# Deformable layer of a four-layer kernel: vertical tent weights made from offsets that DMA lays on every lane

## The chip, the cores and the metric

One NeuronCore of a Trainium2 chip runs the whole program in one launch. The metric is device microseconds of that core, from one execution of the program. Several runs were timed, and one further execution was profiled; durations of single instructions come from the profiled one.

## What is computed

The program chains four layers, each added to its input after a group normalisation of it. Only the first is touched by the change, a deformable 3 x 3 convolution over x of shape 4 images x 128 channels x 128 x 128 pixels:

```
offset = einsum('bchw,oc->bohw', x, w_off) + b_off          # 4 groups x 9 taps x {dy, dx}
py = off[..., dy] + (ky - 1) + row;   px = off[..., dx] + (kx - 1) + column
y0, x0 = floor(py), floor(px);        wy1, wx1 = py - y0, px - x0
val = x at (y0, x0), (y0, x0+1), (y0+1, x0), (y0+1, x0+1), zero outside the image,
      weighted by (1-wy1)(1-wx1), (1-wy1)wx1, wy1(1-wx1), wy1 wx1
out = relu(einsum('bgckhw,ogck->bohw', val, w_def));        x = x + out
```

Each of the 4 groups of 32 channels has its own 9 pairs of offsets at each pixel. The bilinear weight of a sample at distance (dy, dx) from a pixel is the product of two tents, max(0, 1 - |dy|) and max(0, 1 - |dx|). The other layers are a scan along rows, a message layer and a triangle product with layer norms.

## The kernel before, in words

`deform_layer` works in 172 blocks: 4 images x 43 blocks of RY = 3 rows. It replaces the gather by matrix products. For a strip of RX = 4 columns and a block of 3 rows, all samples with offsets below one pixel lie in a patch of SY x SX = 5 x 6 pixels. A *lane* is one pixel of the patch in one group: 30 x 4 = 120 lanes, on 120 partitions.

**Sampling.** `sample` (L521) multiplies, for each of 33 strips, the pixels (`pixels`, lanes x 128 channels, block diagonal in the groups) with the tent weights `m` (lanes x 9 taps x 3 rows x 4 columns), and gives the sampled values in PSUM (`v_ps`). `keep_samples` (L531, L536) copies them to SBUF with ScalarE. `convolved` (L579) then makes the 3 x 3 convolution from the samples, a block later, and `finish` (L552) adds the input.

**Tent weights.** The weight on lane l is the product of a tent along y, made from the tap's dy, and one along x. Both come from TensorE: `places` holds each offset split in three bfloat16 parts, with the parts of max(0, offset) beside them and a row of ones, and `spread` holds small constant matrices that turn these 25 rows into the tents on 120 lanes. `spread_offsets` (L498) does a *round* of such matmuls: for one or two taps, three matmuls along y (one for each row of the block, 130 columns) and four along x (one for each column of a strip, 99 columns) for each tap. The contraction has 25 rows, so that two taps and two directions sit side by side in four row groups of the array. A block takes five rounds (`SLOTS`): two taps four times and one once. `tents` then copies the y tent out of PSUM with ScalarE (`ty`, L508) and multiplies it with the x tent on VectorE (`m`, L510), one tap at a time.

**Preparation.** `prepared` handles 16 rows of an image: it transposes them (L370), scales them and writes a table of pixels to DRAM (`tab`, L378 and L380), makes the offsets with one matmul for each 4 rows (L385 to L393), splits them into parts (L409 to L418), and stores the parts for 8 rows to DRAM (`off`, L423). `counted` takes the statistics of the next image on VectorE. These jobs are generators that advance by one step, or by two where the rows are less than 26 ahead, after each of the eight sample groups of a block.

**Order.** The order on each engine is the order of the program text (`manual_schedule`). In a block, for i = 0 to 7: the round for tents of the next block, the copies of the sample group before, a few convolution matmuls, the sample group i, the products of the round, statistics, a step of preparation. All these loads and stores are DMAs issued by SP, in program order: pixels of the next block (L465, 4 DMAs) at the start of a block, `xres` (L573), the `places` of the block after the next (L449, 8 DMAs) at i = 3, and table and offset stores where the steps come. SP's instructions carry eight semaphores in turn, so that a DMA waits for the one eight before it to have landed.

Of the kernel before, what the change touches and what calls it, by code (L numbers as in the profile page):

```python
# [18 lines left out]
P = 128  # L19
# [30 lines left out]
SLOTS = [(0, 6), (1, 7), (2, 8), (3, 5), (4,)]  # L50
# [130 lines left out]
def deform_layer(tc, c, small, x, w_off, b_off, w_def, x1, tabs, offs):  # L181
# [13 lines left out]
    NB = RY * PADW  # L195
    with ExitStack() as ctx:
        wp = ctx.enter_context(tc.tile_pool(name="l0w", bufs=1))
        ps_g = ctx.enter_context(tc.tile_pool(name="l0ps_g", bufs=1, space=PSUM))
        ps_t = ctx.enter_context(tc.tile_pool(name="l0ps_t", bufs=2, space=PSUM))
        ps_v = ctx.enter_context(tc.tile_pool(name="l0ps_v", bufs=2, space=PSUM))  # L200
# [3 lines left out]
        NPH = NPY + NPX  # L204
# [9 lines left out]
        spread = wp.tile([P, NPH, LANES], BF16, name="spread")  # L214
        places = [wp.tile([P, len(SLOTS), RY, OW], BF16, name=f"places_{i}") for i in range(3)]
# [4 lines left out]
        def rims():  # L220

            zero = two.tile([P, 2 * SX * P], F32, name="zero", tag="m")
            nc.vector.memset(zero, 0.0)
            zrow = zero[0 : NXB + 1]
            zoff = zero[0 : 2 * NL, 0 : NPART * OW].bitcast(BF16)
            zoff = zoff.rearrange("p (n l) -> p n l", n=NPART)
            for b in range(B):
# [14 lines left out]
                nc.scalar.dma_start(rows_[:, :, (S + 2) * OW :], zoff)  # L242

        def tables():

            awayi = two.tile([NG, NPH, LANES], I32, name="awayi", tag="x1c")
            for i in range(NPY):
                nc.gpsimd.iota(
                    awayi[:, i], pattern=[[0, NG], [1, SY], [0, SX]], base=-1 - i,
                    channel_multiplier=0,  # L250
                )
            for i in range(NPX):
                nc.gpsimd.iota(
                    awayi[:, NPY + i], pattern=[[0, NG * SY], [1, SX]], base=-1 - i,
                    channel_multiplier=0,
                )
            away = two.tile([NG, NPH, LANES], F32, name="away", tag="x1c")
# [3 lines left out]
                out=away, in_=away, pattern=[[0, NPH], [1, LANES]], compare_op=ALU.is_ge,  # L261
# [3 lines left out]
                out=away, in_=away, pattern=[[0, NPH], [-1, LANES]], compare_op=ALU.is_ge,  # L265
# [3 lines left out]
            for i, sign in enumerate((-1.0, 1.0, 1.0)):  # L269
                nc.gpsimd.memset(picks[:, i], sign)  # L270
# [17 lines left out]
            for t in (*pixels, parts):  # L288
                nc.gpsimd.memset(t, 0.0)
            yield  # L290
            picks16 = one.tile([NG, 3, P], BF16, name="picks16", tag="ve")
            nc.vector.tensor_copy(picks16, picks.rearrange("g k q r -> g k (q r)"))
            kinds = two.tile([NG, 3, NPH * LANES], BF16, name="kinds", tag="m")
# [10 lines left out]
            n = NPH * LANES // 3  # L304
            for h in range(3):
                if h % 2 == 0:
                    tp = ps_t.tile([P, 2, 512], F32, name="t_ps")
                at = slice(h * n, (h + 1) * n)
                for i in range(3):
                    nc.tensor.matmul(  # L310
                        tp[:, h % 2, 0:n], lhsT=picks16[:, i], rhs=kinds[:, i, at],
                        start=i == 0, stop=i == 2,
                    )
                nc.scalar.copy(to[:, at], tp[:, h % 2, 0:n])
# [43 lines left out]
        def prepared(b, y0):  # L358
# [6 lines left out]
            for h in range(0, RC, RO):  # L365
# [23 lines left out]
                off = one.tile([2 * NL, RO, S], F32, name="off")  # L389
# [14 lines left out]
                def high(t):  # L404
                    halves = t.rearrange("p r c -> p (r c)").bitcast(BF16)
                    return halves.rearrange("p (r c two) -> p r c two", r=RO, two=2)[:, :, :, 1]

                rest = one.tile([2 * NL, RO, S], F32, name="rest")
                nc.scalar.copy(to(0), high(off))  # L409
                nc.gpsimd.tensor_tensor(rest, off, high(off), ALU.subtract)  # L410
                flat = off.rearrange("p r c -> p (r c)")
                nc.vector.tensor_reduce(ranges[:, 0, n : n + 1], flat, AX.X, ALU.max)
                yield
                nc.vector.tensor_reduce(ranges[:, 1, n : n + 1], flat, AX.X, ALU.min)
                nc.scalar.copy(to(1), high(rest))
                nc.gpsimd.tensor_tensor(to(2), rest, high(rest), ALU.subtract)
# [4 lines left out]
                if p0:  # L421
# [5 lines left out]
                        parts,  # L427
# [5 lines left out]
        def shifted(b, d, k, n, row, count):  # L433

            ky, kx = divmod(k, 3)
            wide = (S + 4) * OW
            first = (d * NK + k) * NG * NPART
            whole = offs[b]
            return bass.AP(
                whole.tensor, whole.offset + first * wide + (row - ky + 2) * OW + 2 - kx,  # L440
                [[wide, NG * NPART], [NG * NPART * wide - 1, n], [1, count]],
            )

        def load_places(b, j):
            t = places[(b * NYB + j) % 3]
            for d in range(2):
                for q, slot, k, n in ((0, 0, 0, 3), (0, 3, 3, 2), (1, 0, 6, 3), (1, 3, 5, 1)):
                    p1 = 64 * d + 32 * q + 1
                    nc.sync.dma_start(  # L449
                        t[p1 : p1 + KROWS - 1, slot : slot + n].rearrange("p k r c -> p k (r c)"),  # L450
                        shifted(b, d, k, n, RY * j, RY * OW),
                    )
            if j + 1 == NYB:
                for d in range(2):
                    p1 = 64 * d + 33
                    nc.sync.dma_start(
                        last[p1 : p1 + KROWS - 1].rearrange("p k r c -> p k (r c)"),
                        shifted(b, d, 6, 3, PADW - 1, OW),
                    )
            return t  # L460
# [13 lines left out]
        def spread_offsets(src, slot, taps, rows):  # L474

            tps, todo = [], []
            for q in taps:
                tp = ps_t.tile([P, 2, 512], F32, name="t_ps")
                tps.append(tp)
                for d in range(2):  # L480
                    p0 = 64 * d + 32 * q
                    wide = OW if d else PADW
                    to = tp[0:LANES, d, 0 : rows * wide].rearrange("p (r c) -> p r c", c=wide)
                    mov = src[p0 : p0 + KROWS, slot]
                    if d == 0:
                        ph0 = 0 if rows == RY else RY
                        lot = [(ph0 + r, to[:, r], mov[:, r, 0:PADW]) for r in range(rows)]
                    else:
                        lot = []
                        for i in range(NPX):  # L490
                            cs = slice(i, OW, RX)
                            lot.append((NPY + i, to[:, :, cs], mov[:, :, cs]))
                    todo.append([(p0, *v) for v in lot])
            for i in range(max(map(len, todo))):
                for lot in todo:
                    if i < len(lot):
                        p0, ph, to, mov = lot[i]
                        nc.tensor.matmul(  # L498
# [197 lines left out]
        for i in range(NB_):  # L696
            multiply(advance(i + 1))
# [1149 lines left out]
```

## Time and profile before

| what | value |
|---|---|
| three runs, median (lowest to highest) | 5597.54 us (5583.1 to 5604.08) |
| the profiled execution's own time | 5593.57 us |
| its span, first to last instruction | 5591.7 us |
| granted TensorE clock in it, mean | 0.969 |
| copies `v` out of `v_ps`, L531 | 1376 of 522 ns on ScalarE |
| copies `ty`, L508 | 1548 of 491 ns on ScalarE |
| products `m`, L510 | 1548 of 557 ns on VectorE |
| offset sum on GpSimd, L393 | 128 of 1266 ns |
| pixel loads, L465 | 688 of 123.8 KB |
| loads of `places`, L449 | 1376 of 18.6 to 55.7 KB |
| stores of `off`, L423 | 64 of 891 KB |

How to read the profile: lines of groups give line, engine, operation, output <- input, and a count. In lists of waits, "PE a <- DVE b" is time that TensorE stood before instruction a until VectorE's b was done: microseconds in total, times, longest. In a table of stretches, each engine has its busy time in the stretch with the number of instructions in brackets, in the order PE, PE weight loads, VectorE (DVE), ScalarE (ACT), GpSimd (POOL); the last three columns are the granted clock, the DMA share (mean over 16 engines; packets that overlap on an engine can take it above 1) and GB/s. SPq is SP's queue, with the time that issuing a DMA took. "SP waits" is time in which SP stood in front of a DMA.

### The profile page before, as it was taken

How to read it: one execution, taken by the hardware profiler on the slowest of the kernel's cores; microseconds unless marked ns; L12 is line 12 of the kernel's file. 1: busy time of each engine (PE TensorE's matmuls, PEld its weight loads, DVE VectorE, ACT ScalarE, POOL GpSimd, SP SyncE). 2: the span in 40 equal slices, each digit the busy share in tenths (PEclk: the TensorE clock that was granted, in tenths of full speed). 3: DMA queues.
4: the chain of work that ended last, by engine and by line, in shares of the span. 5: the costliest groups of instructions: out<-in, count | busy, mean ns of one | idle time of the engine just before them, and what ended most of it. 6: DMA issues, size and time to landing. Idle time of an engine off the chain costs nothing. (4 is left out here: it accounts for less than half of the span.)

```text
span 5591.7 us, 112174 instructions
## 1 busy us (share of the span) xinstructions
PE 5190.3 (93%) x42401; PEld 4449.9 (80%) x42401; DVE 3067.1 (55%) x10362; ACT 2766.6 (49%) x5892; POOL 785.0 (14%) x682
## 2 busy tenths in 40 slices
PE   2899999999999999999999989999989889889897
PEld 1778888888888888888888879999957768667687
DVE  6544444554444644444433337888875663754745
ACT  1345555445554455554544432333346574664855
POOL 2022111001111011111100002222200110200202
PEclk9899999999999999999999989999989999999999
DMA  4555555555555546554534322233222451632715
GB/s 142 144 129 137 131 134 119 124 121 136 133 132 117 132 111 138 129 139 107 125 77 79 74 63 84 91 119 94 91 96 86 127 209 36 227 127 78 247 48 172
DMA packets 1138394, 671.45 MB, mean 120 GB/s; under 512 B 737133, under 2 KB 1003566, under 8 KB 1121206
## 3 DMA queue, kind: packets, MB, share of 16 engines
q1 hardware_dynamic: 1127664, 657.77, 44.9%
q8 instruction: 337, 5.52, 0.4%
q10 hardware_dynamic: 10182, 6.43, 0.4%
q14 instruction: 211, 1.73, 0.1%
HBM read 382.88 MB, written 281.11 MB: 119 GB/s over the span
## 5 line engine op out<-in xcount | busy, mean ns | idle before, releaser
L510 DVE TENSOR_TENSOR m<-ty,t_ps 120x390 f32<-120x390 f32 x1548 | 805.2, 557 | 1506.2 <-ACT ty L508 1505.0
L521 PEld LDWEIGHTS v_ps<-m,pixels 120*128 120x128 f32 x11352 | 1442.3, 194 | 86.3 <-issue 9.1
L521 PE MATMUL v_ps<-m,pixels 120*128 120x108 f32 (+1 forms) x11352 | 1467.8, 274 | 3.6 <-ACT v L531 3.5
L531 ACT COPY v<-v_ps 128x432 f32<-128x432 f32 x1376 | 718.8, 522 | 1278.3 <-PE v_ps L521 1275.4
L579 PE MATMUL conv_ps<-v,wdef 128*128 128x128 f32 (+2 forms) x5160 | 1306.5, 380 | 6.5 <-DVE x1c L552 6.0
L579 PEld LDWEIGHTS conv_ps<-v,wdef 128*128 128x128 f32 x5160 | 816.2, 193 | 256.5 <-issue 21.9
L508 ACT COPY ty<-t_ps 120x390 f32<-120x390 f32 x1560 | 688.3, 489 | 175.8 <-PE t_ps L498 168.3
L498 PE MATMUL t_ps<-places,spread 25*120 25x99 bf16 (+1 forms) x10836 | 520.2, 260 | 61.9 <-DVE m L510 38.2
L498 PEld LDWEIGHTS <-spread 25*120 25x120 bf16 x10896 | 338.9, 137 | 224.4 <-issue 124.4
L1605 PEld LDWEIGHTS proj_ps<-wcat,X 128*128 128x128 f32 x4096 | 476.9, 193 | 25.1 <-issue 24.2
L393 POOL TENSOR_TENSOR off<-off,koff 72x512 f32<-72x512 f32 x128 | 162.0, 1266 | 2305.2 <-DVE off L390 2227.2
L1605 PE MATMUL proj_ps<-wcat,X 128*128 128x128 f32 x4096 | 483.8, 277 | 0.1
L1072 ACT ACTIVATE rowT<-x1T_ps,t_x,s_x 128x128 f32<-128x128 f32 x512 | 192.4, 456 | 366.7 <-PE x1T_ps L1065 342.8
L1085 PE MATMUL m_ps<-carry,w 128*128 128x172 f32 x2286 | 361.4, 311 | 0.0
L1699 POOL TENSOR_TENSOR work<-work,gate 128x512 f32<-128x512 f32 x128 | 163.6, 1278 | 1308.4 <-DVE X L1430 842.1
L1085 PEld LDWEIGHTS m_ps<-carry,w 128*128 128x128 f32 x2286 | 345.4, 188 | 0.0
L1614 DVE TENSOR_TENSOR L<-proj_ps,work 128x256 f32<-128x256 f32 x256 | 108.7, 424 | 427.1 <-ACT work L1609 427.1
L1185 POOL TENSOR_TENSOR sum_h<-sum_h,x2c 128x512 f32<-128x512 f32 x128 | 163.0, 1273 | 1159.8 <-DVE x2c L1145 1159.8
L1609 ACT ACTIVATE work<-proj_ps 128x512 f32<-128x512 f32 x256 | 151.5, 597 | 294.4 <-PE proj_ps L1605 291.9
L1710 PE MATMUL out_ps<-outw,work 128*128 128x128 f32 x1024 | 187.6, 285 | 29.0 <-POOL work L1699 27.3
L1710 PEld LDWEIGHTS out_ps<-outw,work 128*128 128x128 f32 x1024 | 159.4, 196 | 40.5 <-POOL work L1699 39.9
L1419 PE MATMUL self_ps<-R,ws 128*128 128x512 f32 x256 | 148.4, 673 | 35.7 <-DVE X L1430 24.3
(236 smaller groups left out, 6561.7 us busy)
## 6 DMA issues: line engine op xcount, KB each, us to landing
pixels<-tab SPq DMA_DIRECT2D x688, 123.8 KB
xin<-in_x_dram SPq DMA_DIRECT2D x56, 1024.0 KB
off<-parts SPq DMA_DIRECT2D x64, 891.0 KB
tab<-rows SPq DMA_DIRECT2D x384, 128.0 KB
places<-off SPq DMA_DIRECT2D x688, 55.7 KB
x<-x1c SPq DMA_DIRECT2D x32, 1024.0 KB
x1rows<-x SPq DMA_DIRECT2D x128, 256.0 KB
x2T<-x2c SPq DMA_DIRECT2D x128, 256.0 KB
```

Of the source, the lines that this page charges most:

```text
L498: nc.tensor.matmul(to, lhsT=spread[p0 : p0 + KROWS, ph, :], rhs=mov, start=True, stop=True,)
L508: nc.scalar.copy(ty[:, 0:n], tp[0:LANES, 0, 0:n])
L510: nc.vector.tensor_tensor(m, ty[:, 0:n].rearrange("p (r c) -> p r c", c=PADW), tx, ALU.mult)
L521: nc.tensor.matmul(vp[:, h * n : h * n + rows * w].rearrange("p (k c) -> p k c", c=w), lhsT=pix[0:LANES, xb, :], rhs=m[:, :, RX * xb : RX ...
L531: nc.scalar.copy(v[:, :, c0 : c0 + 4 * RX].rearrange("p k (h c) -> p k h c", c=RX), vp[:, 0 : 4 * n].rearrange("p (h k c) -> p k h c", h=4 ...
L579: nc.tensor.matmul(pc[:, at : at + r1 - r0, :], lhsT=wdef[:, 3 * ky + kx, :], rhs=v[:, k0 + kx, r0:r1, kx : kx + S], start=m == 0, stop=m ...
L1072: nc.scalar.activation(rt[:, b, :], px[:, b, :], AF.Identity, bias=t, scale=s)
L1085: nc.tensor.matmul(to, lhsT=wgt, rhs=src[:, :, at : at + n], start=i == 0, stop=i + 1 == len(todo),)
L1185: nc.gpsimd.tensor_tensor(sum_h, sum_h, x2c[:, :, i], add)
L1605: nc.tensor.matmul(pp[:, j], lhsT=X[:, j0 + j, :], rhs=wcat[:, cols], start=True, stop=True)
L1699: nc.gpsimd.tensor_tensor(a, a, gt, ALU.mult)
L1710: nc.tensor.matmul(po[:, j], lhsT=a[:, j], rhs=outw, start=False, stop=True)
```

## The change

The y tents no longer come from TensorE. The offsets along y are also written to DRAM as float32 (`offys`, one store for each 4 rows, from a new tile `wide` into which the offsets are now made). For each block, twelve DMAs read them back with a source step of 0 over 30 partitions, so that each lane of a group holds the same offsets, into one of three tiles `tent` (120 lanes x 9 taps x 3 rows x 132 columns, float32). ScalarE then takes |offset + constant of the lane| in place, one instruction for each row (`across`); VectorE makes min(|..| - 1, 0) of the whole tile in place (`lowered`); and `tents` multiplies it in place with the x tent from PSUM, three taps at once. Both factors are negated, so their product is the weight. `places` keeps the x offsets only, in three row groups (one for each ky), loaded by three DMAs; a round of `spread_offsets` makes the x tents of three taps with 12 matmuls, and a block has three rounds. `off` is stored for the x half alone. PSUM: `t_ps` becomes one tile of three banks instead of two tiles of two; `v_ps` three tiles instead of two. The loads for the block after the next move from i = 3 to i = 1.

```diff
+        tent = [wp.tile([LANES, NK, RY, OW], F32, name=f"tent_{i}") for i in range(3)]
...
+                nc.sync.dma_start(
+                    offys[b][:, r0 * OW : (r0 + RO) * OW],
+                    wide[0:NL].rearrange("p r c -> p (r c)"),
+                )
...
-                        parts,
+                        parts[NL:],
...
+        def same_on_lanes(b, g, ky, row, count):
+
+            whole = offys[b]
+            return bass.AP(
+                whole.tensor,
+                whole.offset + (KS * ky * NG + g) * WIDE + (row - ky + 2) * OW + 2,
+                [[0, NS], [NG * WIDE - 1, KS], [1, count]],
+            )
...
-            t = places[(b * NYB + j) % 3]
-            for d in range(2):
-                for q, slot, k, n in ((0, 0, 0, 3), (0, 3, 3, 2), (1, 0, 6, 3), (1, 3, 5, 1)):
...
+            t = places[(b * NYB + j) % 2]
+            y = tent[(b * NYB + j) % 3]
+            for ky in range(KS):
+                for g in range(NG):
                     nc.sync.dma_start(
-                        t[p1 : p1 + KROWS - 1, slot : slot + n].rearrange("p k r c -> p k (r c)"),
-                        shifted(b, d, k, n, RY * j, RY * OW),
+                        y[g * NS : (g + 1) * NS, KS * ky : KS * (ky + 1)].rearrange(
+                            "p k r c -> p k (r c)"
+                        ),
+                        same_on_lanes(b, g, ky, RY * j, RY * OW),
                     )
...
+        def spread_offsets(todo, rows):
+
+            tp = ps_t.tile([P, KS, 512], F32, name="t_ps")
+            for i in range(NPX):
+                cs = slice(i, OW, RX)
+                for q, p0, src in todo:
+                    to = tp[0:LANES, q, 0 : rows * OW].rearrange("p (r c) -> p r c", c=OW)
+                    nc.tensor.matmul(
+                        to[:, :, cs], lhsT=spread[p0 : p0 + KROWS, i, :],
+                        rhs=src[p0 : p0 + KROWS, :, cs], start=True, stop=True,
+                    )
+            return tp
+
+        def across(n, r):
+            t = tent[n % 3][:, :, r]
+            nc.scalar.activation(t, t, AF.Abs, bias=lane_y[:, r : r + 1])
+
+        def lowered(t):
+            nc.vector.tensor_scalar(t, t, 1.0, 0.0, ALU.subtract, ALU.min)
 
         def tents(tp, m, rows):
 
-            n = rows * PADW
-            ty = two.tile([LANES, NB], F32, name="ty")
-            nc.scalar.copy(ty[:, 0:n], tp[0:LANES, 0, 0:n])
-            tx = tp[0:LANES, 1, 0 : rows * OW].rearrange("p (r c) -> p r c", c=OW)[:, :, 0:PADW]
-            nc.vector.tensor_tensor(
-                m, ty[:, 0:n].rearrange("p (r c) -> p r c", c=PADW), tx, ALU.mult
-            )
+            tx = tp[0:LANES, :, 0 : rows * OW].rearrange("p k (r c) -> p k r c", c=OW)
+            nc.vector.tensor_tensor(m, m, tx, ALU.mult)
...
             for i in range(NG_X):
-                if i == 3:
+                if i == 1:
                     load_row(n + 2)
-                todo = advance(NB_ * (n + 1) + DONE[i])
+                todo = []
+                if more and i in (2, 4, 6):
+                    todo.append((n + 1, i // 2 - 1, spread_row(n + 1, i // 2 - 1)))
...
-                multiply(todo)
...
+                for v_ in todo:
+                    multiply(*v_)
+                if more and i == 0:
+                    across(n + 1, RY - 1)
+                if more and i == 1:
+                    lowered(tent[(n + 1) % 3])
+                if n + 2 < len(blocks) and i in (6, 7):
+                    across(n + 2, i - 6)
```

## The prediction, as put on record before the changed kernel ran

> **What bounds the kernel now.** I read the page first: its span, the engines' shares and the slices, to see which part of the span the change reaches.
>
> ```profile
> span 5591.7 us, 112174 instructions
> PE 5190.3 (93%) x42401; PEld 4449.9 (80%) x42401; DVE 3067.1 (55%) x10362; ACT 2766.6 (49%) x5892; POOL 785.0 (14%) x682
> ...
> PE   2899999999999999999999989999989889889897
> DMA  4555555555555546554534322233222451632715
> ```
>
> The deformable layer fills the first 23 to 24 of the 40 slices (its last sampling copy ends at 3303 us). TensorE is busy there in nine tenths or more of each slice, VectorE and ScalarE in about half. DMA stands at about half too, against two tenths in the next layer. So a DMA that is added lands where DMA is already fullest.
>
> Next, TensorE's own waits, from 440 us (past the ramp) to 3300 us:
>
> ```profile
> PE t_ps L498 <- DVE m L510: 13.6, 26, 2.6
> ...
> PE t_ps L498 <- DMA places<-off: 3.0, 5, 0.7
> ```
>
> Under 25 us of waits in 2860 us: in this stretch the layer's time is TensorE's list of work. Between the small closing copies of `keep_samples` (L536), which mark the blocks, I count 54 blocks without preparation of offsets (median 16.7 us), 97 with it (mean 18.2), 13 in the ramp (mean 21.9, the first ones held by VectorE's statistics) and the blocks at the ends of images. Then the timeline of TensorE, to price one round of `spread_offsets`:
>
> ```profile
> 1515.31 0.27 PE L370 MATMUL img_ps<-ident,xin 128*128 128x128 f32 x1
> 1515.52 0.56 PE L498 MATMUL t_ps<-places,spread 25*120 25x130 bf16 x14
> 1516.00 1.34 PE L579 MATMUL conv_ps<-v,wdef 128*128 128x384 f32 x4
> 1517.18 1.04 PE L521 MATMUL v_ps<-m,pixels 120*128 120x108 f32 x8
> 1518.16 0.55 PE L498 MATMUL t_ps<-places,spread 25*120 25x130 bf16 x7
> 1518.64 1.13 PE L579 MATMUL conv_ps<-v,wdef 128*128 128x256 f32 x4
> ```
>
> A round of 14 small matmuls stands between the last transpose, started at 1515.31, and the convolution at 1516.00. The transpose's own turn is 0.11 (four in 0.60, the last 0.27 long), so the round costs 0.58 us. A round of 7 costs the same: the eighth v_ps starts at 1517.18 + 1.04 - 0.26 = 1517.96, its turn ends at 1518.07, the next convolution starts at 1518.64, so 0.57. A round has a price, whatever number of matmuls is in it.
>
> Last, what DMA can carry: stretches of the trace (the last two columns are DMA share and GB/s), and SP's timeline in one block.
>
> ```profile
> 1531.00:1535.40 4.40, 4.40 (x36) 3.25 (x36) 0.76 (x2) 2.33 (x5) 0.00 (x0) 1.00 0.76 214
> 1542.00:1544.50 2.50, 2.50 (x22) 2.45 (x21) 1.88 (x4) 1.54 (x4) 1.81 (x2) 1.00 1.26 165
> 1540.60:1558.60 18.00, 18.00 (x169) 15.00 (x173) 7.55 (x14) 9.78 (x21) 4.31 (x4) 1.00 0.65 148
> 3200.00:3216.70 16.70, 16.70 (x162) 14.39 (x161) 5.22 (x11) 8.04 (x18) 0.00 (x0) 1.00 0.33 64
> ```
>
> ```profile
> 1540.61 2.23 SPq L465 DMA_DIRECT2D pixels<-tab  x4
> 1542.94 0.66 SPq L573 DMA_DIRECT2D xres<-in_x_dram  x1
> 1543.64 3.45 SPq L449 DMA_DIRECT2D places<-off  x8
> ```
>
> The stretches are one store of offsets; one load of pixels; one block with preparation; one without. In the store only 12 of 16 engines work (share 0.76) and they move 214 GB/s; all 64 such stores are near it (432 packets of 2112 B, mostly in 4.6 to 5.0 us, so 180 to 200). SP issues a DMA of `places` every 0.41 us. Over 440 to 3300 us SP waits 648 us for TensorE before pixel loads: 3.9 us of spare time in each of 166 blocks.
>
> **The change, part by part.**
>
> TensorE. Five rounds a block become three (12 matmuls each, 36 instead of 63). At 0.58 that is 2 x 0.58 = 1.16 us a block, x 172 = 200 us; at each image's end three rounds become one, 8 x 0.57 = 5. If nothing else moved: -205 us.
>
> ScalarE. Nine copies `ty` of 0.49 us go (4.4 a block). Three Abs over 1188 elements come. Copies of 130 and 390 elements took 268 and 491 ns, so 0.86 ns an element and 157 ns fixed; with up to 0.2 for the bias (the 512-wide ACTIVATE at L373 took 786, the copies 600): 1.2 to 1.4 us each, 3.6 to 4.2 a block. No change.
>
> VectorE. Nine products of 557 ns (5.0) become three of 1188: from 291 and 557 ns at 130 and 390 elements, 1.4 each, 4.1. New is `lowered`, 3564 elements in float32: 3.7 us at the products' 1.02 ns an element, 1.9 at half of that; bf16 at L418 took 0.44. At most +2.8 on 7.6 us busy in an 18 us block. Behind it queue six bn_stats (1.3 us) and the first product. With one `t_ps` buffer instead of two, the second round (i=4, some 8 us into the block) waits for that product, due 7 to 9 us in: 0 to 1 us in the one block of five that counts statistics, up to 30 us; I take 10. PSUM's third `v_ps` buffer lets TensorE run about two sample groups (4 us) past a ScalarE that is held up.
>
> DMA: this decides. A block's tents are 120 lanes x 9 taps x 1584 B = 1.71 MB, in 12 loads of 90 packets. The pixels, the largest load now, are 0.51 MB. Out go half of `places` (0.17 MB) and half of the offset store. How fast will 1584-byte packets to 30 lanes run? From both sides: the row nearest in packet size is `xres` (1536 B, 128 lanes). Its packets took 65 to 79 ns at the median; 1080 of them on the 15 engines that such a load uses are 4.7 to 5.7 us. But the Trainium skill ("SBUF — State Buffer", Door 1: The DMA port swizzle) says that a transfer's rate hangs on how many of SBUF's 16 ports its partitions reach: 32 partitions, and 64 as well, reach eight, measured there at 189 GB/s for 1 MiB against 328 for 128 partitions. By that rule it is 9.1 us. The row that speaks for it is the store above, from 72 lanes, at 180 to 214. I take 200 GB/s: 8.6 us. No row shows 30 lanes reading one and the same DRAM row, as these loads do. That can't beat the packet time, and may be slower.
>
> Then the waits on SP. In SP's program of the changed kernel the store of `offy` waits for the tents' loads of the same image in flight to land, and in most blocks it follows them directly; all later DMAs queue behind it: table rows, offset store, next pixels. A small `places` load, issued at 1511.36, had landed at 1513.11, so about 1.4 us pass between the end of issuing and landing.
>
> The queue for two blocks with preparation (it runs one step per i, so about one `offy` a block, six `tab` and one offset store every two):
> - pixels 2 x 0.51 MB at 165 GB/s: 6.2; xres 1.0
> - tents 2 x 8.6: 17.2; places 2 x 0.17 MB at 200: 1.7
> - offy 2 x 0.4, and 2 x 1.4 for landing: 3.6
> - tab 6 x 0.61: 3.7; offset store 0.46 MB at 200: 2.3
> - xin and x1, 0.9 of 1 MB in 2.7 us (128 packets of 8192 B went at 48 per us): 2.4
>
> Together 38.1, or 19.0 us a block. TensorE would need 18.2 - 1.2 = 17.0. So these blocks become the queue's, +0.8 us each: 97 x 0.8 = +78. Blocks without preparation: 3.1 + 0.5 + 8.6 + 0.9 + 1.4 = 14.5 us, below TensorE's 15.5, so they gain: 54 x 1.16 = -63; the images' ends -12. In the ramp six blocks write two `offy` and six `tab` each: about 3 us more, +18; the first tents, before the first sample, +5. Abs waits for the tents on ScalarE at i=6; queued behind it are the copies out of `v_ps` and the scaling of table rows, for which SP then waits. The copies are covered by the 4 us above; for the rows I take 1 us in every fourth prepared block, +24. With VectorE's 10: 78 - 63 - 12 + 18 + 5 + 24 + 10 = +60, less about 10 where x1 stores overlap table issues: +50 us. The profiled execution took 5593.6 us (span 5591.7); the median of the runs is 5597.5, 4 us above. On the median: 5650.
>
> **Rivals.**
> 1. TensorE stays the bound (the other side). If the tents run at xres's packet rate, 10.4 us for two blocks in place of 17.2, the queue needs 31.3, or 15.7 a block, less than 17.0. The 205 us come through but for some 10 to 40 us of starts and waits: 5390 to 5430. The turning point is the tents' rate: +50 vanishes when two blocks' queue is 1.0 us shorter, that is at about 212 GB/s; at 260 the queue needs 34.1 for two and TensorE decides. For it: loads to lanes 0-59 and 60-119 may drift apart and share all ports, and the loads are free of the offset store's small rows. Against it: the store at 214, and how fixed that is.
> 2. The shared source row is a hot spot: 15 engines reading the same 1584 B. At 120 GB/s tents take 14.3, prepared blocks 24.7 and the others 20: +800 us. Nothing in the trace speaks for it; nothing shows a broadcast either.
> 3. VectorE or the single `t_ps` becomes the bound: at worst 7.6 + 2.8 of 17 us, so it can't set the pace; 30 us at most, inside the ranges.
>
> **How the numbers follow.** The queue sets the pace (tents at 175 to 220 GB/s), 5580 to 5820: 0.55, of which 0.12 within 0.5% (28 us, about what a measurement of this kernel tells from no change) and 0.01 faster. TensorE the bound or nearly, 5385 to 5565: 0.33. Hot spot, above 5820: 0.12. Faster 0.34, same 0.12, slower 0.54. The range leaves some 0.08 at each end: 5400 to 5850; the likeliest case alone has 5580 to 5820.
>
> **What would show it.** Right: t_ps rounds at 0.58 us, three a block; blocks without preparation at 15.5 us; with preparation near 19, TensorE waiting there for v_ps copies or `m`, ScalarE for the tents' DMA, SP on `offy` for tents; DMA share above 0.85 in such a block; tents near 200 GB/s. Wrong: prepared blocks at 17 us with TensorE full, or blocks without preparation above 16.7. That last would mean that the tents' loads alone take over 10 us.

## The result, and the profile after

The changed kernel took 5886.51 us, median of 4 runs (5877.17 to 5895.4); the kernel before, beside it, 5592.44 (5583.1 to 5604.08). The ratio is 1.0527, 95% interval 1.0508 to 1.0547: 294 us slower, where 50 slower was forecast, outside the range. The profiled execution has a span of 5875.4 us, 283.7 more than before.

The page after, with the slices:

```profile
span 5875.4 us, 103049 instructions
...
PE 5107.6 (87%) x37747; PEld 4411.5 (75%) x37747; DVE 3319.1 (56%) x9499; ACT 2687.0 (46%) x4850; POOL 797.2 (14%) x683
...
PE   2688889989889888899889997999998989889797
...
DMA  5778778787788787788787873323323171441715
```

The last sampling copy ends at 3584.8 us instead of 3303.3, so 281.5 of the 283.7 us lie in the deformable layer. There the row of PE has fallen from 9 to 8 and 9, and DMA has gone from 5 to 7 and 8. The stretches show the same in numbers; the first is 500 us of the layer, the second the loading of one block's tents alone:

```profile
2500.00:3000.00 500.00, 453.99 (x3504) 388.17 (x3502) 255.75 (x428) 231.44 (x381) 75.91 (x72) 0.92 0.81 187
...
3306.00:3313.00 7.00, 6.88 (x59) 5.51 (x58) 2.92 (x3) 1.57 (x3) 0.00 (x0) 1.00 0.92 202
```

TensorE is busy for 454 us (426 to 454 in the five such stretches from 500 on; 493 to 498 before) at a granted clock of 0.90 to 0.92 (0.97 to 1.00 before). The tents come at 202 GB/s; in the single microseconds in which nothing but tents moves, the median is about 195. The forecast's 200 GB/s is there. DMA's share is 0.92 while the tents come, and 0.8 over 500 us: as a whole it is not full.

By blocks, counted between the closing copies as in the forecast (us, mean; the same block numbers in both, sorted by the kernel before):

| blocks | before | after | together | forecast |
|---|---|---|---|---|
| 97 with preparation | 18.19 | 20.00 | +175 | +102 (78 and 24) |
| 54 without (median 16.7, now 18.0) | 16.97 | 18.45 | +80 | -63 |
| 13 in the ramp | 21.93 | 24.69 | +36 | +18 |
| 7 at images' ends | 26.4 | 25.2 | -8 | -12 |

The new instructions cost what was forecast (last number ahead of the second bar: mean ns of one; behind it idle time, and what ended it):

```profile
L531 DVE TENSOR_TENSOR tent<-tent,t_ps 120x1188 f32<-120x1188 f32 x516 | 715.9, 1387 | 600.7 <-PE t_ps L515 593.8
L523 ACT ACTIVATE tent<-tent,lane_y 120x1188 f32<-120x1188 f32 x516 | 665.0, 1289 | 607.1 <-DMA places<-off 296.7
L526 DVE TENSOR_SCALAR tent<-tent 120x3564 f32<-120x3564 f32 x172 | 355.0, 2064 | 675.1 <-ACT tent L523 463.1
```

Product 1.39 us, Abs 1.29, `lowered` 2.06. The column behind the second bar is the news: ScalarE idled 607 us in front of Abs, about as long as Abs itself ran. The waits of the layer past the ramp (440 to 3585 us), TensorE's, ScalarE's and SP's:

```profile
PE off_ps L394 <- ACT rows L382: 124.6, 35, 10.9
PE v_ps L540 <- ACT v L550: 80.9, 39, 7.4
PE t_ps L515 <- DVE tent L531: 72.7, 48, 3.6
...
ACT tent L523 <- DMA places<-off: 282.9, 68, 12.3
ACT tent L523 <- DMA tent<-offy: 116.2, 23, 11.5
...
SPq L499 <- PE v_ps L540: 261.5, 72, 14.5
SPq L423 <- DMA tent<-offy: 193.5, 113, 4.9
```

TensorE, which waited under 25 us for all of this before, now waits for table rows of ScalarE, for ScalarE's copies and for VectorE's product. Each of the three stands behind Abs, on ScalarE itself or on VectorE, which waits for it. ScalarE's wait named "places" is put down to the load that came last; Abs reads no `places`, and the tents' loads are issued between them. SP's last line is the store of `offy` behind the tents.

A block without preparation shows how it fits together. TensorE's timeline first: the eighth v_ps of a group starts at 3301.97 + 1.04 - 0.26 = 3302.75, its turn ends at 3302.86, the convolution starts at 3303.43. A round of 12 costs 0.57 us, as forecast. Then the block after it:

```profile
3301.97 1.04 PE L540 MATMUL v_ps<-tent,pixels 120*128 120x108 f32 x8
3302.94 0.56 PE L515 MATMUL t_ps<-places,spread 25*120 25x99 bf16 x12
3303.43 0.71 PE L598 MATMUL conv_ps<-v,wdef 128*128 128x128 f32 x4
...
3315.04 1.28 ACT L523 ACTIVATE tent<-tent,lane_y 120x1188 f32<-120x1188 f32 x1 [3.12 <-DMA tent<-offy]
3316.64 1.28 ACT L523 ACTIVATE tent<-tent,lane_y 120x1188 f32<-120x1188 f32 x1
3318.32 1.30 ACT L523 ACTIVATE tent<-tent,lane_y 120x1188 f32<-120x1188 f32 x1
3319.65 2.02 DVE L526 TENSOR_SCALAR tent<-tent 120x3564 f32<-120x3564 f32 x1 [5.90 <-ACT tent L523]
3321.77 1.39 DVE L531 TENSOR_TENSOR tent<-tent,t_ps 120x1188 f32<-120x1188 f32 x1
3323.22 0.56 PE L515 MATMUL t_ps<-places,spread 25*120 25x99 bf16 x12 [1.44 <-DVE tent L531]
```

The pixels of that stretch were issued from 3299.47 on, when TensorE had left the block before; then `xres`, then the tents. The last tents landed at 3314.97, 15.5 us later. The queue's part of a block is the forecast's 14.5 us, nearly. But TensorE has used up its block by then. From the landing to the second round it is 8.3 us more: three Abs with copies between them, `lowered`, product, in a row. The pixels of the next block wait for TensorE again, so this is a loop: SP issues when TensorE is done, and TensorE waits for what SP issued last.

### The profile page after: what moved, and what is told of

The parts are those of the page before. It is cut to its first block, busy times and chain, and to the rows that moved or that the text cites. A ratio compares the mean times of both kernels' runs of the same rounds, so it can differ in the third digit from the quotient of the medians.

```text
span 5875.4 us, 103049 instructions
## 1 busy us (share of the span) xinstructions
PE 5107.6 (87%) x37747; PEld 4411.5 (75%) x37747; DVE 3319.1 (56%) x9499; ACT 2687.0 (46%) x4850; POOL 797.2 (14%) x683
## 5 line engine op out<-in xcount | busy, mean ns | idle before, releaser
L540 PEld LDWEIGHTS v_ps<-tent,pixels 120*128 120x128 f32 x11352 | 1502.7, 201 | 195.4 <-ACT v L550 101.8
L540 PE MATMUL v_ps<-tent,pixels 120*128 120x108 f32 (+1 forms) x11352 | 1527.1, 282 | 95.3 <-ACT v L550 93.2
L598 PEld LDWEIGHTS conv_ps<-v,wdef 128*128 128x128 f32 x5160 | 861.7, 203 | 301.3 <-issue 62.4
L531 DVE TENSOR_TENSOR tent<-tent,t_ps 120x1188 f32<-120x1188 f32 x516 | 715.9, 1387 | 600.7 <-PE t_ps L515 593.8
L523 ACT ACTIVATE tent<-tent,lane_y 120x1188 f32<-120x1188 f32 x516 | 665.0, 1289 | 607.1 <-DMA places<-off 296.7
L526 DVE TENSOR_SCALAR tent<-tent 120x3564 f32<-120x3564 f32 x172 | 355.0, 2064 | 675.1 <-ACT tent L523 463.1
L402 POOL TENSOR_TENSOR offwide<-offwide,koff 72x512 f32<-72x512 f32 x128 | 141.0, 1102 | 2542.9 <-DVE offwide L399 1996.4
L515 PE MATMUL t_ps<-places,spread 25*120 25x99 bf16 x6192 | 302.2, 287 | 112.9 <-DVE tent L531 93.2
L515 PEld LDWEIGHTS <-spread 25*120 25x120 bf16 x6240 | 205.0, 149 | 213.9 <-issue 157.3
L394 PE MATMUL off_ps<-xin,woff 128*72 128x512 f32 x256 | 162.4, 721 | 144.5 <-ACT rows L382 144.5
```

Source lines behind the costliest of these rows:

```text
L515: nc.tensor.matmul(to[:, :, cs], lhsT=spread[p0 : p0 + KROWS, i, :], rhs=src[p0 : p0 + KROWS, :, cs], start=True, stop=True,)
L523: nc.scalar.activation(t, t, AF.Abs, bias=lane_y[:, r : r + 1])
L526: nc.vector.tensor_scalar(t, t, 1.0, 0.0, ALU.subtract, ALU.min)
L531: nc.vector.tensor_tensor(m, m, tx, ALU.mult)
L540: nc.tensor.matmul(vp[:, h * n : h * n + rows * w].rearrange("p (k c) -> p k c", c=w), lhsT=pix[0:LANES, xb, :], rhs=m[:, :, RX * xb : RX ...
L598: nc.tensor.matmul(pc[:, at : at + r1 - r0, :], lhsT=wdef[:, 3 * ky + kx, :], rhs=v[:, k0 + kx, r0:r1, kx : kx + S], start=m == 0, stop=m ...
```

## Experiments

Four theories are tried. Q: SP's queue is too long, by bytes and by its waits. L: tents land too late for where Abs stands in ScalarE's order, and ScalarE and VectorE hold up TensorE from there. E: the new work on ScalarE and VectorE costs by itself. P: loads to 30 neighbouring lanes run at part of the DMA rate. The changed kernel has 5886.5 throughout, and blocks are sorted as in the table above. Runs without an interval are single ones. The four runs of the changed kernel span 18 us, and the kernel before, timed anew beside each group of runs, took 5580 to 5592, so that a difference under some 20 us says nothing.

**No loads of tents.** They are loaded for the first three blocks only; later blocks work on what lies in the tiles.

```diff
-                for g in range(NG):
+                for g in range(NG if b * NYB + j < 3 else 0):
```

> The twelve tent loads are issued for the first three blocks only; later blocks go on with what is left in the three tent tiles, so the weights along y are not the reference's. All other instructions stay. Theory Q (the DMA queue: bytes and SP's waits set the pace) and theory L (the tents land too late for Abs, and ScalarE holds up TensorE) both put the loss on the loads: 5390 to 5450 us, blocks without preparation at 15.5 us, granted clock back at 0.97. Rival E (the new work on ScalarE and VectorE and the single t_ps buffer cost the time, whatever the loads do): above 5600 us.

Measured: 5328.67 us beside 5583.24 for the kernel before (0.954). Blocks without preparation 15.24 us (median), with it 16.52 (mean). The granted clock is 0.971. So the saving on TensorE is real, 255 us. The Abs, `lowered` and products are all still there, and past the ramp (440 to 3050 us) TensorE waits 9 us for them, so theory E falls:

```profile
PE t_ps L515 <- DVE tent L531: 9.2, 9, 2.6
```

The loads cost 558 us.

**No Abs.** Abs and `lowered` of the blocks are left out; the loads stay.

```diff
-                if more and i == 0:
-                    across(n + 1, RY - 1)
-                if more and i == 1:
-                    lowered(tent[(n + 1) % 3])
-                if n + 2 < len(blocks) and i in (6, 7):
-                    across(n + 2, i - 6)
```

> Abs and the lowering are left out in the blocks (the products take the raw offsets), all loads stay. The first instruction that needs the tents is then the product on VectorE at i=2 of the next block, some 8 us later than Abs at i=6. Theory Q: the queue is as long as before, so prepared blocks stay at 19 to 20 us and only the others fall to 15.5: 5700 to 5750 us. Theory L: ScalarE never stands before tents, so all blocks gain: 5480 to 5600 us.

Measured: 5674.1 us, between the answers of Q and L. Blocks with preparation are at 18.96 us (mean; median 17.29), near the forecast queue's 19.0. Blocks without it have a median of 15.24, the same as with no loads at all, but a mean of 17.09, no less than before (16.97). They are of two kinds: the 30 at the end of the last image fall from 16.72 to 15.59 (mean), the other 24 rise from 17.29 to 18.97. The waits of TensorE (440 to 3400 us) have lost those for copies and table rows:

```profile
PE t_ps L515 <- DMA places<-off: 82.8, 47, 3.1
PE img_ps L379 <- DMA xin<-in_x_dram: 53.9, 12, 8.5
...
PE t_ps L515 <- DVE tent L531: 24.6, 21, 2.9
```

Eighteen of the 24 lie in or beside the stretches where the next image is read for its statistics (`xin`, 1 MB a load). One such stretch, with seven of these loads, is from 1110 to 1260 us (waits of VectorE and of TensorE):

```profile
DVE stats L343 <- DMA xin<-in_x_dram: 36.9, 5, 13.2
PE conv_ps L598 <- DVE x1c L571: 22.4, 4, 12.0
```

VectorE stands before the statistics until `xin` has landed, x1c stands behind them in its order, and TensorE's convolution waits for x1c.

Taking away work that costs next to nothing when the tents are there gains 212 us here: with it go ScalarE's wait for late tents and the time of Abs and `lowered` between landing and product. That is L's part. The other 345 us of the 558 are there without any Abs; they are put down to Q.

**Tents ahead of the pixels.**

```diff
+            load_row(n + 2)
             if n + 1 < len(blocks):
                 pixel_tiles[n + 1] = load_pixels(*blocks[n + 1])
...
-                if i == 1:
-                    load_row(n + 2)
```

> The tents and places of the block after the next are loaded ahead of the next block's pixels instead of behind them (some 4 us earlier in the queue); bytes and instructions are the same. Theory Q: prepared blocks unchanged, 5780 to 5880 us. Theory L: Abs at i=6 finds its tents 4 us sooner, most of ScalarE's 490 us in front of Abs go, and TensorE's waits with them: 5600 to 5720 us.

Measured: 5811.74 us, 75 less, in the range that Q had. Blocks with preparation fall from 20.00 to 19.47 (mean), the others from 18.45 to 18.31. TensorE waits somewhere new (440 to 3500 us), and VectorE ahead of it:

```profile
PE conv_ps L598 <- DVE x1c L571: 215.2, 83, 11.0
...
DVE x1c L571 <- DMA xres<-in_x_dram: 308.1, 86, 9.4
```

The load of `xres` now stands behind tents and pixels.

**The store of offy from GpSimd's queue.**

```diff
-                nc.sync.dma_start(
+                nc.gpsimd.dma_start(
                     offys[b][:, r0 * OW : (r0 + RO) * OW],
```

> The store of the y offsets is issued by GpSimd instead of SP, so that its wait for the tents' loads no longer stands in SP's queue (SP waited 211 us there, 119 times). Theory Q: prepared blocks 1.5 to 2 us shorter, 5700 to 5750 us. Theory L: the loads start earlier only in prepared blocks, by up to 1.8 us: 5780 to 5850 us. If the wait on GpSimd delays the preparation instead: no gain.

Measured: 5917.74 us, 31 more than the changed kernel. SP no longer stands 194 us in front of this store, and nothing comes of it: prepared blocks are at 20.45. But GpSimd now stands in front of it (idle time behind the second bar), with the rest of the preparation behind it:

```profile
L423 POOL DMA_DIRECT2D offy<-offwide x128 | 79.7, 623 | 442.9 <-DMA places<-off 289.1 <-DMA tab<-rows 73.4 <-DMA tent<-offy 44.1
```

So the wait was moved, not removed, and what SP's standing costs by itself is not shown.

**A third of the bytes.** Twelve loads as before, of one tap each after the first three blocks (n = 1 instead of 3); two of three taps keep old contents.

```diff
-                    [[0, NS], [NG * WIDE - 1, KS], [1, count]]
+                    [[0, NS], [NG * WIDE - 1, n], [1, count]]
```

> Twelve tent loads a block as in the changed kernel, but each brings one tap instead of three (0.57 MB a block instead of 1.71); the other taps go on with old contents, so the weights along y are not the reference's. If the bytes set the pace: near the run without loads, 5340 to 5420 us. If the number of loads and SP's issuing and waiting set it: above 5600 us.

Measured: 5493.49 us, 393 less, with the number of loads as it was; between the two answers. Blocks without preparation 15.24 (median), with it 17.75 (mean). Bytes (and with them the time until the last tents land) are most of the 558; what is left over "no loads" is 165. The median packet took 67 ns instead of 111 (mean 98 instead of 114), so packets went faster where fewer of them were under way.

**Lanes spread over the partitions.** Lane = place x 4 + group, so a load writes every fourth partition; the pixels and the constants of the lanes are laid in the same order.

```diff
-                        y[g * NS : (g + 1) * NS, KS * ky : KS * (ky + 1)].rearrange(
+                        y[g:LANES:NG, KS * ky : KS * (ky + 1)].rearrange(
...
-                        me[g * NS : (g + 1) * NS], same_on_lanes(b, g, KS - 1, PADW - 1, OW)
+                        me[g:LANES:NG], same_on_lanes(b, g, KS - 1, PADW - 1, OW)
```

> The 120 lanes are ordered by (place, group) instead of (group, place), so that a load for one group goes to every fourth of 120 partitions instead of 30 neighbours; pixels are loaded the same way. Bytes, packets and instructions are the same. Theory P[...]: tents at 280 GB/s or more, 5 to 6 us a block instead of 8.5, and 5380 to 5480 us, below the kernel before. If the common source row or the number of packets sets the rate: unchanged, 5850 to 5900 us.

Measured: 6298.31 us, ratio to before 1.1279 (1.1259 to 1.1299), much slower. Packets took 67 ns at the median (101 in the mean, 114 in the changed kernel), but DMA's share fell to 0.66 at 164 GB/s. SP's timeline says why:

```profile
3214.99 3.46 SPq L474 DMA_DIRECT2D tent<-offy  x4
3218.50 0.53 SPq L480 DMA_DIRECT2D places<-off  x1
```

Four strided loads took 3.46 us to issue; in the changed kernel four took 1.73 to 2.53. Past the ramp SP was issuing for 3029 of 3560 us here, for 1965 of 3145 there. SP could not issue fast enough, and this run says little on P.

**Own rows.** Each lane reads a DRAM row of its own, so the numbers are not the tap's offsets.

```diff
-                whole.offset + (KS * ky * NG + g) * WIDE + (row - ky + 2) * OW + 2,
-                [[0, NS], [NG * WIDE - 1, KS], [1, count]],
+                whole.offset + (g % 2) * WIDE + (row - ky + 2) * OW + 2,
+                [[WIDE, NS], [2 * WIDE - 1, KS], [1, count]],
```

> Each lane reads a DRAM row of its own instead of all 30 lanes of a group reading one; sizes and targets are the same, the offsets along y are then not the reference's. Theory P: no change, 5850 to 5900 us. The rival of a hot source row: tents faster, below 5700 us.

Measured: 5848.27 us, packets 111 ns as with the shared row. The shared row costs some 38 us by this single run; the hot spot (rival 2), put at 800, falls.

**Spread lanes, tents ahead of the pixels.** The two edits above together.

> The lanes of e6 and the order of loads of e3 together (tents ahead of pixels). Theory P with theory L: if tents still come late for some Abs in e6, this takes the rest away: 5340 to 5450 us, at or below e6. If the pixels are then late: above e6.

Measured: 6196.14 us, 1.1085 (1.1067 to 1.1104): 102 less than spread alone, far from the 5340 to 5450 expected, and bound by issuing like it (SP: 2907 of 3478 us). TensorE waited 448 us for x1c, that is for `xres`.

**Four loads instead of twelve.** `offy` is stored with the rows of each ky displaced, so that nine taps lie at one step.

```diff
-            for ky in range(KS):
-                for g in range(NG):
+            for g in range(NG):
...
-                        same_on_lanes(b, g, ky, RY * j, RY * OW),
+                    same_on_lanes(b, g, 0, RY * j, RY * OW, NK),
...
-                [[0, NS], [NG * WIDE - 1, KS], [1, count]],
+                [[0, NS], [NG * WIDE - 1, n], [1, count]],
```

> The changed kernel with the offsets along y stored so that the nine taps lie at one step (the rows of each ky displaced by 129 numbers in DRAM): four loads of 9 taps take the place of twelve of 3, with the same bytes, the same 1584-byte packets and the same lanes; a block issues 11 DMAs for rows of tents and pixels instead of 19. If bytes and packets set the queue (theory Q in its plain form), nothing moves: 5860 to 5900 us, packets 111 ns, DMA share in the layer 0.79 to 0.82. If a good part of what is paid is for each load (issuing and its fixed time: with a third of the bytes the loads still cost some 165 us), the time falls by 80 to 165 us, to 5720 to 5800, and blocks without preparation fall from 18.0 (median) to about 17. A rise would mean that twelve loads share out the engines better than four.

Measured: 5953.0 us, 1.0662 (1.0645 to 1.068). Fewer loads are slower, by 67 us; packets 129 ns, tents 190 GB/s. SP was issuing for 1708 us past the ramp instead of 1965 and nothing came of it, so its time to issue is not what is paid. Of the number of loads alone the run says less, since the packets became slower with it. The forecast of a gain was wrong.

**Four loads, spread.** Both edits; eight strided DMAs a block instead of sixteen.

> Four loads as in the run beside it, with the lanes in the order (place, group), so that a load writes every fourth partition. With twelve loads this order brought packets from 111 to 67 ns but doubled SP's issue of each from 0.41 to 0.83 us, and the kernel was slower (1.128). Here only eight strided DMAs a block are left (four of tents, four of pixels), 8 x 0.83 + 3 x 0.41 = 7.9 us of issuing instead of 16. Theory P ([...]time of packets is what is paid): the loads cost (67/111) of 558 us instead of all of it, so 5330 + 340 = 5670, 5600 to 5720; less if the number of loads counts too. If what is paid is bytes whatever the ports, or if a strided issue holds the engines as well as SP: 5850 or more, and packets above 67 ns.

Measured: 5897.95 us, 1.0565 (1.0544 to 1.0585). Packets 105 ns, tents 227 GB/s instead of 190. Spreading the lanes makes the tents 1.19 times as fast and the kernel 55 us faster than four loads to neighbouring lanes. P is real, but a fifth and not a half, and it only pays for what four loads lost. Whether neighbouring lanes do so well because several loads are in flight at once, each to other lanes, was not tested.

**Four loads, spread, tents first.**

> As the run beside it with the loads of tents ahead of the pixels of the next block, which took 75 us off the changed kernel and 102 off the spread one with twelve loads. If the tents' late landing still sets the block (theory L), 60 to 100 us below the run beside it, and 5550 to 5650 if that is 5650 to 5720: level with the kernel before. If the pixels are now what comes late, no gain or a loss, and TensorE's waits stand at the convolution (table rows and x1c) instead of at the tents.

Measured: 5837.12 us, 1.0466 (1.0446 to 1.0486), 61 less than the run beside it; TensorE waits 236 us for x1c. The order of the queue gives its gain again, the lanes give none on top of it (twelve loads, tents first: 5812).

**Tents and xres ahead of the pixels.** As "tents ahead", with the load of `xres` issued at the end of the block before.

```diff
-                convs = convolved(b, *terms_of(j, before, v), stats, 3, 2)
+                what = terms_of(j, before, v)
+                convs = convolved(b, *what, stats, 3, 2, xres_of(b, what[0], what[1]))
```

> Tents ahead of the pixels took 75 us off the changed kernel, but TensorE then stood 215 us before convolutions, for VectorE's x1c, which waits for the load of xres that now stands behind tents and pixels. Here xres is issued ahead of both, at the end of the block before. If the order of the queue is what is left to repair, most of those 215 us go: 5610 to 5680, and no wait of TensorE above 60 us at the convolution. If the queue as a whole is full (theory Q: some 1.9 MB a block in 18 us), the wait only changes its place, to the tents or the pixels: 5760 to 5820.

Measured: 5760.88 us, 1.0311 (1.0291 to 1.033): the fastest with all the loads, 126 below the changed kernel. The wait for x1c fell from 215 us to 51, as the first answer had it, but the time is the second answer's, at its lower edge. The waits of TensorE (440 to 3500 us):

```profile
PE v_ps L540 <- DMA pixels<-tab: 66.9, 30, 6.1
PE img_ps L379 <- DMA xin<-in_x_dram: 63.0, 10, 10.8
PE conv_ps L602 <- DVE x1c L571: 50.6, 14, 10.1
```

Now pixels and images come late: the wait has changed its place. DMA's share is 0.80 to 0.87 in 500-us stretches.

**Later Abs.** The order of loads of the changed kernel; all three Abs stand in the block that uses them.

```diff
                 if more and i == 0:
-                    across(n + 1, RY - 1)
+                    for r in range(RY):
+                        across(n + 1, r)
...
-                if n + 2 < len(blocks) and i in (6, 7):
-                    across(n + 2, i - 6)
```

> The changed kernel with the later Abs alone, its loads in their own order. Two of the three Abs wait about half a block less, so that ScalarE no longer stands in front of them with the copies of the samples behind it. Leaving Abs and lowered out altogether took 212 us off. If the place of the Abs in ScalarE's order is the fault, 100 to 160 us come back: 5730 to 5790. If the tents are late for any place before the first product, the wait moves from the copies (TensorE before v_ps and off_ps) to the second round (before t_ps): 5850 to 5930.

Measured: 5808.79 us, 1.0405 (1.0386 to 1.0425), 78 less. Short of the 100 to 160 expected: TensorE's waits for copies (17 us) and table rows (58) shrink, but

```profile
PE t_ps L515 <- DVE tent L531: 150.5, 110, 3.6
```

the second round now waits twice as long for the product. The place of Abs is worth 78 us. The other 134 of the 212 stay: the tents are late wherever Abs stands, and Abs and `lowered` still lie between their landing and the product.

**Both.**

> As the run beside it, with all three Abs of a block's tents in the block that makes them into weights (at its first sample group) in place of two of them one block earlier; lowered and the rounds stay. If ScalarE held up by late tents still costs time (theory L), 20 to 80 us below the run beside it. If the tents now land in time, three Abs in a row (3.9 us) before the copies of sample groups use up the third v_ps buffer: 0 to 60 us above.

Measured: 5774.81 us, 1.0328 (1.0308 to 1.0348), level with the earlier Abs (5760.88; the intervals overlap). With the tents early, the later Abs has nothing to give.

## Why the prediction was wrong

Two steps failed: what waits behind the tents on ScalarE was put at 24 us, and the queue of blocks without preparation left out the loads of the next image. The terms in turn:

- **TensorE's saving** (-205): right in sign and in the price of a round. Without the loads the kernel gained 255. Blocks without preparation went to 15.24 us, 0.3 lower than two rounds explain; I did not look for the reason.
- **ScalarE and VectorE by themselves** (no change; +10): right. All three durations are as forecast, and with the loads gone TensorE waits 9 us for them.
- **The tents' rate** (200 GB/s, 8.6 us a block): right, 195 to 202. The packet row of `xres` (65 to 79 ns) would have given 4.7 to 5.7 us and the Trainium skill's port rule ("SBUF — State Buffer", Door 1: The DMA port swizzle) 9.1; at 195 GB/s it is 8.8. Yet lanes that by that rule reach all ports moved 1.19 times as much as 30 neighbouring ones with four loads, and not the 1.7 of its table.
- **The queue of a prepared block** (19.0 us): right as a mean where no Abs stands in the way. Without Abs, these blocks took 18.96. They are uneven (median 17.29), which a sum over two blocks doesn't show.
- **Abs behind the tents** (+24): failed, and this is the larger part. The step is "Abs waits for the tents on ScalarE at i=6 ... The copies are covered by the 4 us above; for the rows I take 1 us in every fourth prepared block, +24". Removing Abs and `lowered` gave 212 us. TensorE's waits past the ramp name the terms: table rows 125 us where 24 stood, copies 81 where they were called covered, the product 73 where 10 stood. I compared two lengths, 14.5 us of queue with 15.5 of TensorE, as if the queue began where it liked. It begins when TensorE leaves a block, since the pixels wait for that, and ends 15.5 us later; Abs, `lowered` and product are another 8.3 us behind it. ScalarE stood up to 12.3 us in front of an Abs, three times the 4 us of cover. The bound called "wrong" in the forecast (above 16.7) was read there as loads that alone take over 10 us. They don't; it is the chain behind them.
- **Blocks without preparation** (-63; a queue of 14.5 us, below TensorE's 15.5): failed even without Abs. The sum has `xin` for prepared blocks only, yet 14 loads of the next image's statistics fall into these. At the forecast's own 2.7 us a load that is 38 us of queue, an estimate. With no Abs the 30 blocks at the end of the last image gained 34 us, as forecast; the 24 others lost 40, where the forecast had them gain 28. How much of that is `xin` was not tested apart.
- **The sum**: with Abs left out, blocks come to +74 (with preparation), +6 (without), +20 (ramp) and -15 (ends), where the forecast had +78, -63, +23 and -12. Its total without the +24 and the product's +10 was 5616, and the run took 5674. Of the 236 us between 5650 and 5886, then, 178 are the chain behind the tents and 58 the rest, nearly all in blocks without preparation.
- **The clock**, which had no term. From 150 us to the last sampling copy, in the order before, after, no loads, no Abs:

```profile
150.00:3303.30 3153.30, 3100.85 (x28184) 2616.42 (x28184) 1468.72 (x4245) 1596.34 (x3487) 411.56 (x370) 0.98 0.53 119
150.00:3584.80 3434.80, 3025.83 (x23576) 2582.10 (x23576) 1720.60 (x3390) 1513.28 (x2454) 425.58 (x368) 0.92 0.79 180
150.00:3040.40 2890.40, 2833.00 (x23576) 2440.55 (x23577) 1714.33 (x3390) 1530.06 (x2454) 438.59 (x368) 0.98 0.46 114
150.00:3385.80 3235.80, 2964.03 (x23571) 2544.50 (x23569) 1378.91 (x3218) 956.87 (x1942) 386.27 (x366) 0.94 0.84 191
```

By the profile TensorE was idle for 52 us before and 409 after (the second number less the third), and its busy time fell by 75 us, where the forecast took 205 off its list. The difference went into slower matmuls: the granted clock was at one half for 126 us before (15 stretches) and 570 after (80), and two v_ps matmuls started 213 ns apart in them instead of 112. Summed over the layer such longer steps come to about 60 us before and 220 after. With no loads the half-clock time is 96 us, with no Abs 403, with tents and xres first 434. It goes with the waits in every run here; no run changed the clock alone. So it is no third part of the loss: it lies inside the two parts of the sum, as what the waits cost besides themselves. Of the 545 us that the loads cost in the layer, 352 are idle time and 193 longer busy time.

Of the rivals, the first (TensorE the bound) came true only without the loads, the second (a hot source row) fell by the run with own rows. The third was wrong as put (VectorE is busy for half of the time), but its single `t_ps` is where the late product stops TensorE.

Settled: the loads cost 558 us; their bytes are 393 of it; 212 go through Abs and `lowered`, of which 78 belong to the place of Abs; the order of the queue is worth 126. These overlap and don't add up: order and place together gave no more than order alone. The 345 us that stay without Abs are, in the layer, 214 of idle time and 131 of longer busy time against no loads. Open: which load each part of that idle time is owed to, and whether a fourth tile of tents or a third of pixels (a block more of lead), or a second queue for the tents, would hide it. None of these was tried.

## What to carry to other kernels

A load that is issued when the bounding engine leaves a block and used in the next has that block's time for everything: transfer, landing and each step behind it, in a row. Add these up from the issue to the first use, and don't compare the sum of transfers with the engine's time alone. Make the list of loads for each kind of block, with those that come only now and then. A wait for a DMA put into an in-order engine that also frees PSUM for TensorE holds up all that stands behind it; try the version without the loads and the version without the waiting instruction, which together tell lateness from work. And count a wait of TensorE twice where the granted clock falls with it: once as idle time, once in the matmuls after it.

## What the runs showed of the hardware

- SP's issue of a load whose target is every fourth partition took 0.82 us (median of the tents' loads), where one to 30 neighbouring partitions took 0.41. Pixel loads went the same way, from 0.63 to 0.85.
- Four loads of 270 packets ran slower than twelve of 90 with the same bytes: 129 ns a packet (median) against 111, 190 GB/s against 195, and the kernel took 67 us more.
- Thirty lanes reading one and the same DRAM row were about as fast as with 30 rows: 111 ns a packet both ways.
- The half clock comes in pieces of 3.41 us or a multiple of it (3.41 to 17.07 in the layer after). From 2900 to 3300 us TensorE had ten idle gaps of 1.7 us or more. At eight of them, seven of 1.7 to 2.6 us and one of 4.0, such a piece began within 2 us of the gap's end; at two, of 2.1 and 2.4 us, none did. The Trainium skill ("TensorE: Matmul & The Clock Gate", What's actually happening) has half rate after an idle window of about 3.4 us; here shorter gaps were enough seven times, and not enough twice.
